# Transposing x one iteration ahead in a two-layer graph kernel

## The chip, the cores and the metric

The kernel runs on one core of a Trainium2 chip. Its time is the device time of one execution in microseconds (us); the median of several runs is given with the lowest and the highest. The engines are named as in the profile: PE is TensorE (matmuls and transposes), PEld its weight loads, DVE VectorE, ACT ScalarE, POOL GpSimd, SP SyncE. POOL and SP also issue DMAs; all data is float32 except some small index tables in bfloat16.

## The reference

```python
# x 4096 x 512, adj 4096 x 4096: about 0.2% of it and the diagonal are not zero,
# these entries lie between 0.05 and 1
a = adj + eye                                  # layer 0
d = sum(a, axis=1) ** (-0.5)
out = relu(((d[:, None] * a * d[None, :]) @ x) @ W.T + b)
x = layernorm(x + out)

adj = maximum(adj, eye)                        # layer 1: 8 heads, key size 64
q, k, v = x @ Wqs, x @ Wks, x @ Wvs            # for each head
scores = q @ k.T * 64 ** (-0.5) + 0.01 * eye - 1e16 * (1 - adj)
x = layernorm(x + sum over heads of softmax(scores) @ v @ Wo)
```

The test of the data that the kernel makes on the chip allows a shorter form. With all weights below 1, each off-diagonal score of layer 1 lies hundreds of millions below the diagonal's, so softmax is 1 on the diagonal and layer 1 is `layernorm(x + x @ (Wv @ Wo))`. With at most 9 neighbours handled as columns beside the diagonal in a row (after a redistribution in the tile), layer 0 is a sum of a few gathered rows of `y = d * (x @ W.T)`. The function that does this is `few_edges_below_one` (L420); a general path stands behind it and isn't run on this data.

## The kernel before, in words

The 4096 rows are worked on in 32 tiles of 128. Two passes follow each other.

**First pass**, the loop `for t in range(NT + 1)` (L1053 to L1095). In iteration t:

- SP loads the adjacency tile t + 3 (2 MB, `load_first` L561). 14 early tiles and the last 5 go into the 5 buffers of `big` (`a_t`) and stay until DVE has scanned them; the other 13 pass through the 2 buffers of `pn` (`a_n`), are only summed, and are loaded again later (`reload` L993).
- ACT sums the rows of tile t (`sum_rows` L710), or, for early tiles, only its negative part (L715). POOL turns the sums into `d` (`scaling`, L722 to L725); for early tiles `d` comes from DVE's scan (L970).
- x tiles are multiplied with W. `prefetch` (L1041) fetches one x tile by a POOL DMA (L550) into one of 6 buffers, `transpose_rows` (L689) transposes an x tile on PE into one of 3 PSUM buffers (`pt`), `evacuate` (L694) copies it by ACT into one of 2 buffers (`xT`), and `times` (L703) makes the product on PE into one of 5 PSUM buffers (`acc`). When `d` of that tile is known, `keep_y` (L727) scales the product on ACT (L736) and stores it to `y` in DRAM by a POOL DMA (L738).
- DVE scans an adjacency tile: 8 times MAX8 (L752) and FIND_INDEX8 (L753) on 512 columns each, 9 of its 16 steps in each iteration (`RATE`), and sorts what it found (L774 to L783). `match` (L910) hands surplus neighbours of full rows to other rows of the tile, in stages on DVE and PE: KEY, ACROSS (a transpose on PE, L855), RANKS (DVE, L864), PERM (L872), MOVE (matmuls, L881 and L884), END (DVE, L892 to L899).
- Setup steps (second-layer weights) stand between, one in an iteration that has fewer than two x tiles to turn.

The list `due` (L1031) holds for each x tile the iteration in which its product is scaled. `projected(t)` (L1027) says up to which due iteration products are made in iteration t: t + 1, and one more from each iteration in `SOONER` on. Each engine works in its own order, as the program is written out and a scheduler has laid it; some instructions are pinned to program order (ACT's `keep_y` and, in the last 7 iterations, the copies of `evacuate`).

**Second pass** (from L1101). For each tile, 9 indirect gathers on POOL (L1113, 128 rows of `y`, 256 KB each; 19 buffers, 18 ahead) fetch neighbour rows. ACT builds a scaled permutation matrix for each (`spread`, L1006 to L1019), PE multiplies and adds (L1326); in most tiles some gathers are first added together on ACT (L1130) and DVE (L1132, `presum`). Then DVE adds the own part (`scaled` L1183), applies relu and adds x (`residual` L1191), and layer 1's product and normalisation follow. Beside that DVE goes on with the scan of the reloaded tiles, and SP loads `y` and x rows (L1123) and reloads adjacency tiles.

Of the kernel before, what the change touches and what calls it, by code (L numbers as in the profile page):

```python
# [419 lines left out]
def few_edges_below_one(  # L420
# [20 lines left out]
    H, _, KD = wks.shape  # L441
    NT = N // P
# [33 lines left out]
    p1 = first.enter_context(tc.tile_pool(name="first", bufs=2))  # L476
# [71 lines left out]
    def load_x(t, engine, pool, bufs):  # L548
        x_t = pool.tile([P, D], FP, name="x_t", bufs=bufs)
        engine.dma_start(x_t, x[ts(t, P), :])  # L550
        return x_t
# [9 lines left out]
    def load_first(t, parts=1):  # L561
        if t in early or t in resident:
            return load_a(t, parts=2 if t == NT - 1 else parts)
        return load_a(t, pn, "a_n")
# [10 lines left out]
    wT = p1.tile([P, ND, D], FP, name="wT", bufs=1)  # L575
# [25 lines left out]
    def load_second_weights():  # L601

        nc.sync.dma_start(
            wv.rearrange("p (h f) -> p h f", h=H),
            wvs.rearrange("h (p j) k -> p h (j k)", j=ND),
        )
        su1 = p1.tile([P, 2, ND, D], FP, name="wo", bufs=1)
        nc.sync.dma_start(su1[:, 0], wo.rearrange("(r a) k o -> (a k) r o", a=2))
        return su1

    def order_second_weights():
        nc.gpsimd.tensor_copy(
            w_nat.rearrange("p j (h k) -> p j h k", h=H),
            wv.rearrange("p (h j k) -> p j h k", h=H, j=ND),
        )
# [70 lines left out]
    def transpose_rows(src, dcs=range(ND)):  # L686
        pt = ps_t.tile([P, 512], FP, name="pt")
        for dc in dcs:
            nc.tensor.transpose(pt[:, ts(dc, P)], src[:, ts(dc, P)], ident)  # L689
        return pt  # L690

    def evacuate(pool, name, pt, pinned=False):
        dst = pool.tile([P, ND, P], FP, name=name, bufs=2)
        copy = nc.scalar.copy(dst.rearrange("p c s -> p (c s)"), pt[:, :D])  # L694
        if pinned:
            tc.keep_in_program_order(copy)
        return dst

    def times(srcT, w, u=None, dcs=range(ND)):
        if u is None:  # L700
            u = ps_a.tile([P, D], FP, name="acc")
        for dc in dcs:
            nc.tensor.matmul(  # L703
                u, srcT[:, dc, :], w[:, dc, :], start=(dc == 0), stop=(dc == ND - 1)
            )
        return u

    def sum_rows(dst, part):
        dump = wk_.tile([P, N], mybir.dt.uint8, name="dump")
        nc.scalar.activation(dump[:, : part.shape[1]], part, AF.Copy, accum_out=dst)  # L710

    def sum_negative(t, a_t, halves=(0, 1)):
        dump = wk_.tile([P, N], mybir.dt.uint8, name="dump")
        o = slice(halves[0] * N // 2, (halves[-1] + 1) * N // 2)
        nc.scalar.activation(  # L715
            dump[:, o], a_t[:, o], AF.Relu, scale=-1.0,
            accum_out=neg_all[:, t, halves[0] : halves[0] + 1],
        )

    def scaling(t, more=None):  # L720
        deg = small.tile([P, 1], FP, name="deg")
        nc.gpsimd.tensor_scalar(deg, deg_all[:, t : t + 1], 1.0, None, op0=ALU.add)  # L722
        if more is not None:
            nc.gpsimd.tensor_tensor(deg, deg, more, ALU.add)
        nc.gpsimd.tensor_tensor(d_all[:, t : t + 1], deg, mhalf, ALU.pow)  # L725

    def keep_y(t, u):  # L727
        if t in due_first:
            y_t = p1.tile([P, D], FP, name="y_t", bufs=4)
        else:  # L730
            if not y_bank:
                y_bank.append(p1.tile([P, 8, D], FP, name="wo", bufs=1))
            y_t = y_bank[0][:, y_count[0] % 8]
            y_count[0] += 1
        tc.keep_in_program_order(
            nc.scalar.activation(y_t, u, AF.Copy, scale=d_all[:, t : t + 1])  # L736
        )
        nc.gpsimd.dma_start(y[ts(t, P), :], y_t)  # L738
# [171 lines left out]
    def match(*stages):  # L910
        for stage in stages:
            n = staged[stage]
            if stage == KEY:
                ready = n < len(sorted_)
            elif stage == PERM:
                ready = n < staged[RANKS] and n - staged[MOVE] < 2
            else:
                ready = n < staged[stage - 1]
            if stage == ACROSS:
                ready = ready and n == staged[RANKS]  # L920
            if stage == MOVE:
                ready = ready and n == staged[END]
            if not ready:
                continue
            t = order[n]
            e = edges[t]
            if stage == KEY:
                e["key"] = match_key(t)
            elif stage == ACROSS:
                e["pk"] = match_across(e["key"])  # L930
            elif stage == RANKS:
                e["rank"] = match_ranks(e["key"], e["pk"])
            elif stage == PERM:
                e["perm"] = match_perm(e["rank"])
            elif stage == MOVE:
                e["pm"] = match_move(e["rec"], e["perm"])
            else:
                match_end(t, e["pm"])
                matched.add(t)
            staged[stage] += 1  # L940
# [44 lines left out]
    def some(upto):  # L985
        while count[0] < upto:
            count[0] += 1
            next(work, None)
# [33 lines left out]
    xs, us = {}, {}  # L1022
    DEEP = 3
    RATE = 9
    SOONER = (17, 21, 25)

    def projected(t):  # L1027

        return t + 1 + sum(t >= e for e in SOONER)

    due = [(t + 1, t) for t in range(NT) if t not in early]  # L1031
    for n, t in enumerate(early):
        at = max(t + 3, -(-STEPS * (n + 1) // RATE) + 1)
# [7 lines left out]
    def prefetch(count):  # L1041
        for _ in range(count):
            if fetch:
                t = fetch.pop(0)
                xs[t] = load_x(t, nc.gpsimd, p1, 6)

    prefetch(5)
    for t in range(1, DEEP):
        a_tiles[t] = load_first(t)
# [2 lines left out]
    setup, left = iter(()), None  # L1052
    for t in range(NT + 1):  # L1053
        if t == 0:
            su1 = load_second_weights()
        if t + DEEP < NT:
            a_tiles[t + DEEP] = load_first(t + DEEP)
        if t == 3:
            order_second_weights()
            setup = second_weights(su1)  # L1060

        lo, hi = projected(t - 1) + 1, projected(t)
        ahead = [j for at, j in due if lo <= at <= hi]
        pts = []
        for j in ahead:
            prefetch(1)
            pts.append(transpose_rows(xs.pop(j)))
        kind, begin, end = next(setup, (None,) * 3) if len(ahead) < 2 else (None,) * 3
        got = begin() if kind == "t" else None
        if t < NT:  # L1070
            if t in early:
                sum_negative(t, a_tiles[t])
            else:
                sum_rows(deg_all[:, t : t + 1], a_tiles[t][:, : N // 2 if t == NT - 1 else N])
                more = None
                if t == NT - 1:
                    more = small.tile([P, 1], FP, name="more")
                    sum_rows(more, a_tiles[t][:, N // 2 :])
                scaling(t, more)
            if t in again:  # L1080
                del a_tiles[t]
        if left:
            left()
            left = None
        for j in [j for at, j in due if at == t]:
            keep_y(j, us.pop(j))
        for j, pt in zip(ahead, pts):
            us[j] = times(evacuate(p1, "xT", pt, t >= NT - 7), wT)
        if kind == "t":
            end(got)  # L1090
        if kind == "p":
            left = lambda end=end, pa=begin(): end(pa)
        if t < NT - 5:
            match(*ALL)
        some((t + 1) * RATE)  # L1095
# [170 lines left out]
    yo, zs, hs, pts, hTs, ws, sts, mats, halves = ({} for _ in range(9))  # L1266
# [28 lines left out]
    for i in range(NT + 2):  # L1295
# [6 lines left out]
        for k in range(KH):  # L1302
            ends = p == NT - 1
            t = at("T", i, k)
            if t not in (None, NT - 1):
                hTs[t] = evacuate(p2, "hT", transpose_rows(hs[t]))
            t = at("M", i, k)
# [48 lines left out]
            t = at("Q", i, k)  # L1356
# [3 lines left out]
            t = at("V", i, k)  # L1360
# [4 lines left out]
            t = at("F", i, k)  # L1365
# [45 lines left out]
```

## Time and profile before

| what | us |
|---|---|
| median of 3 runs | 639.45 (638.96 to 639.71) |
| the profiled execution | 641.63 |
| its span in the trace | 639.8 |
| busy PE / DVE / ACT / POOL | 529.4 / 556.3 / 498.3 / 357.6 |
| first gather of the second pass starts | 228.90 |
| mean granted clock of PE | 0.947 |

The profiled execution is 2.2 us above the median of the runs. In timelines a line has start, duration, engine, line of the kernel, operation, output and inputs, number of instructions put together, and in brackets the idle time before it with what ended it. In windows a line has the stretch, its length, busy time and number of instructions on PE, PEld, DVE, ACT and POOL, PE's granted clock, the share of time that the 16 DMA engines are busy, and GB/s.

### The profile page before, as it was taken

The page shows a single profiled execution, that of the slowest core. Times are in us where ns is not written, and L with a number is a line of the kernel's source. Part 1 is how long each engine was busy: PE and PEld are TensorE (multiplying, and loading weights), DVE is VectorE, ACT ScalarE, POOL GpSimd, SP SyncE. Part 2 cuts the span into 40 slices and gives each one's busy share as a digit, 9 for nine tenths or more (in the row PEclk, how much of TensorE's full clock was granted, in tenths as well). Part 3 has the DMA queues.
Part 4 walks back from the last instruction along what each step waited for, and adds up shares of the span by engine and source line. Part 5 has one row for each costly group of instructions (what it writes and reads, how often), then busy time and mean ns, then how long its engine had stood idle before and what let it go on. Part 6 is the DMA issues. An engine that isn't in the chain of part 4 may idle for free. (4 is left out here: it accounts for less than half of the span.)

```text
span 639.8 us, 7790 instructions
## 1 busy us (share of the span) xinstructions
PE 529.4 (83%) x1537; PEld 241.9 (38%) x1537; DVE 556.3 (87%) x2037; ACT 498.3 (78%) x1093; POOL 357.6 (56%) x465
## 2 busy tenths in 40 slices
PE   1599876589896636898897989999999999988884
PEld 1354333244443212344333433444444444433332
DVE  5699999999999995899988989999999999644431
ACT  0868667798876877699878888898998999857732
POOL 5222222232432167777777757676777777777730
PEclk9999987799998859799997989999999999989998
DMA  9999999899999378999999999999999888887851
GB/s 329 402 422 422 423 425 427 319 422 422 425 427 417 136 250 257 341 397 397 399 396 399 399 400 384 373 325 341 381 366 292 279 245 298 274 271 247 280 160 38
DMA packets 57273, 217.68 MB, mean 340 GB/s; under 512 B 8701, under 2 KB 9981, under 8 KB 52864
## 3 DMA queue, kind: packets, MB, share of 16 engines
q1 hardware_dynamic: 23888, 115.48, 45.6%
q0 software_dynamic: 28192, 92.30, 41.0%
q10 hardware_dynamic: 5136, 9.31, 3.9%
q8 instruction: 14, 0.23, 0.2%
q14 instruction: 43, 0.35, 0.1%
HBM read 200.28 MB, written 16.78 MB: 339 GB/s over the span
## 5 line engine op out<-in xcount | busy, mean ns | idle before, releaser
L1113 POOL DMA_INDIRECT g<-y,cols_all x288 | 287.3, 998 | 101.9 <-issue 46.2
L1326 PE MATMUL acc<-g,s_t 128*128 128x512 f32 x450 | 222.1, 625 | 31.4 <-DMA x_t<-in_x_dram 14.6
L752 DVE MAX8 v_all<-a_t 128x8 f32<-128x512 f32 x256 | 166.9, 681 | 14.8 <-DMA a_t<-in_adj_dram 14.8
L753 DVE FIND_INDEX8 idx<-v_all,a_t 128x8 uint32<-128x512 f32 x256 | 173.7, 687 | 0.0
L703 PE MATMUL acc<-wT,xT 128*128 128x512 f32 x256 | 124.9, 641 | 26.4 <-ACT xT L694 26.4
L1326 PEld LDWEIGHTS acc<-g,s_t 128*128 128x128 f32 x450 | 83.1, 197 | 122.7 <-issue 75.3
L703 PE MATMUL acc<-wvo,hT 128*128 128x512 f32 x256 | 116.9, 598 | 3.2 <-ACT hT L694 2.3
L715 ACT ACTIVATE dump<-a_t 128x2048 uint8<-128x2048 f32 (+1 forms) x50 | 119.1, 2383 | 0.0
L703 PEld LDWEIGHTS acc<-wT,xT 128*128 128x128 f32 x256 | 50.8, 206 | 88.6 <-issue 57.3
L703 PEld LDWEIGHTS acc<-wvo,hT 128*128 128x128 f32 x256 | 48.6, 192 | 65.5 <-issue 57.1
L1006 ACT ACTIVATE sq<-cols,wr_all 128x128 f32<-128x128 f32 x160 | 58.7, 393 | 15.1 <-DMA a_t<-in_adj_dram 12.8
L1132 DVE SCALAR_TENSOR_TENSOR g<-g,wr_all 128x512 f32<-128x512 f32 x58 | 43.2, 745 | 29.4 <-ACT g L1130 17.4
L1010 ACT ACTIVATE s_t<-sq,wr_all 128x128 f32<-128x128 f32 x128 | 58.3, 485 | 0.5
L722 POOL TENSOR_SCALAR deg<-deg_all 128x1 f32<-128x1 f32 x32 | 7.2, 227 | 90.9 <-DVE deg_all L970 52.2
L710 ACT ACTIVATE dump<-a_n 128x4096 uint8<-128x4096 f32 x13 | 47.2, 3634 | 0.0
L1130 ACT ACTIVATE g<-g,wr_all 128x512 f32<-128x512 f32 x31 | 22.1, 714 | 29.7 <-DMA g<-y,cols_all 22.5
L550 POOL DMA_DIRECT2D x_t<-in_x_dram x32 | 18.0, 563 | 41.3 <-PE pt L689 31.9
L783 DVE MAX8 top<-key 128x8 f32<-128x64 f32 x192 | 36.0, 214 | 0.1
L694 ACT COPY xT<-pt 128x512 f32<-128x512 f32 x32 | 18.4, 593 | 19.2 <-PE pt L689 12.4
L774 DVE SCALAR_TENSOR_TENSOR key<-key,top 128x64 f32<-128x64 f32 x128 | 32.3, 274 | 0.0
L689 PE MATMUL pt<-ident,x_t 128*128 128x128 f32 x128 | 19.9, 289 | 9.4 <-DMA x_t<-in_x_dram 8.9
L1183 DVE SCALAR_TENSOR_TENSOR h<-yo,own_all,acc 128x512 f32<-128x512 f32 (+1 forms) x33 | 23.7, 719 | 4.0 <-PE acc L1140 4.0
(135 smaller groups left out, 660.8 us busy)
## 6 DMA issues: line engine op xcount, KB each, us to landing
a_t<-in_adj_dram SPq DMA_DIRECT2D x17, 2048.0 KB, 20.1
a_t<-in_adj_dram SPq DMA_DIRECT2D x56, 512.0 KB, 14.2
a_n<-in_adj_dram SPq DMA_DIRECT2D x13, 2048.0 KB, 14.4
x_t<-in_x_dram POOLq DMA_DIRECT2D x32, 256.0 KB, 11.3
yo<-y SPq DMA_DIRECT2D x32, 256.0 KB, 5.8
x_t<-in_x_dram SPq DMA_DIRECT2D x32, 256.0 KB, 6.6
out_dram<-r_t ACTq DMA_DIRECT2D x31, 256.0 KB, 4.9
y<-y_t POOLq DMA_DIRECT2D x18, 256.0 KB, 10.8
```

What stands on the lines that cost most here:

```text
L703: nc.tensor.matmul(u, srcT[:, dc, :], w[:, dc, :], start=(dc == 0), stop=(dc == ND - 1))
L710: nc.scalar.activation(dump[:, : part.shape[1]], part, AF.Copy, accum_out=dst)
L715: nc.scalar.activation(dump[:, o], a_t[:, o], AF.Relu, scale=-1.0, accum_out=neg_all[:, t, halves[0] : halves[0] + 1],)
L752: long.append(lambda o=o, seg=seg: nc.vector.max(v[:, o], seg))
L753: long.append(lambda o=o, seg=seg: nc.vector.max_index(idx[:, o], v[:, o], seg))
L774: return lambda: nc.vector.scalar_tensor_tensor(out, a, sc, b, op0=op0, op1=op1, **kw)
L783: return lambda: nc.vector.max(top[:, f, r * 8 : r * 8 + 8], keyf[:, f])
L1006: nc.scalar.activation(sq, cols1, AF.Square, bias=wr[:, 2, k : k + 1])
L1010: nc.scalar.activation(s_t[:, k, :], away(), AF.Relu, scale=wr[:, 3, k : k + 1], bias=wr[:, 1, k : k + 1],)
L1113: nc.gpsimd.indirect_dma_start(out=slots[j], out_offset=None, in_=y[:, :], in_offset=bass.IndirectOffsetOnAxis(ap=cols_all[:, t, k : k + 1 ...
L1132: nc.vector.scalar_tensor_tensor(g, slots.pop(i * KH + k), w, g, op0=ALU.mult, op1=ALU.add)
L1326: nc.tensor.matmul(zs[i], mats[i][:, KH if k < summed[i] > 1 else k, :], slots.pop(i * KH + k), start=False, stop=(k == KH - 1),)
```

## The change

`SOONER` becomes (13, 16, 19): the product runs two, three and four due iterations ahead from iterations 13, 16 and 19 on, instead of 17, 21 and 25. From iteration 14 (`LEAD`) on, a tile of x is transposed one iteration before the one in which it is copied and multiplied: `turn_rows` is called where the transposes stood (up to 3 transposed tiles in hand) and again behind the iteration's products (up to 2 in hand). Each transpose still fetches one more x tile. What is multiplied in an iteration is still set by `projected(t)`.

```diff
-    SOONER = (17, 21, 25)
+    SOONER = (13, 16, 19)
...
+    LEAD = 14
+    turned, done = {}, [0, 0]
+
+    def turn_rows(upto, most):
+
+        while done[0] < upto and done[0] - done[1] < most:
+            j = due[done[0]][1]
+            prefetch(1)
+            turned[j] = transpose_rows(xs.pop(j))
+            done[0] += 1
...
-        lo, hi = projected(t - 1) + 1, projected(t)
-        ahead = [j for at, j in due if lo <= at <= hi]
-        pts = []
-        for j in ahead:
-            prefetch(1)
-            pts.append(transpose_rows(xs.pop(j)))
-        kind, begin, end = next(setup, (None,) * 3) if len(ahead) < 2 else (None,) * 3
+        ahead = sum(at <= projected(t) for at, _ in due)
+        turn = sum(at <= projected(t + (t >= LEAD)) for at, _ in due)
+        turn_rows(turn, 3)
+        kind, begin, end = next(setup, (None,) * 3) if ahead - done[1] < 2 else (None,) * 3
...
-        for j, pt in zip(ahead, pts):
-            us[j] = times(evacuate(p1, "xT", pt, t >= NT - 7), wT)
+        while done[1] < ahead:
+            j = due[done[1]][1]
+            us[j] = times(evacuate(p1, "xT", turned.pop(j), t >= NT - 7), wT)
+            done[1] += 1
+        turn_rows(turn, 2)
```

Written out, the x tiles multiplied in each iteration, and those transposed in it after the change, are:

| iteration | products before | products after | transposes after |
|---|---|---|---|
| 13 | 11 | 11, 14 | 11, 14 |
| 14 | 14 | 13 | 13, 16 |
| 15 | 13 | 16 | 15, 18 |
| 16 | 16 | 15, 18 | 17 |
| 17 | 15, 18 | 17 | 20 |
| 18 | 17 | 20 | 19, 22 |
| 19 | 20 | 19, 22 | 21 |
| 20 | 19 | 21 | 24 |
| 21 | 22, 21 | 24 | 23 |
| 22 | 24 | 23 | 26 |
| 23 | 23 | 26 | 25, 27 |
| 24 | 26 | 25, 27 | 28 |
| 25 | 25, 27, 28 | 28 | 29 |
| 26 | 29 | 29 | 30 |
| 27 | 30 | 30 | 31 |
| 28 | 31 | 31 | |

In the changed kernel lines behind the loop of the first pass have a number that is 11 higher. The products held in PSUM until their `d` is known are at most 5, the number of buffers, in both: in iterations 25 to 27 before, 24 to 27 after.

## The prediction

> **What bounds the kernel now.** I read the busy tenths of the whole span first, then the timelines of PE, ACT, POOL and DVE where the first pass ends (183 to 268 us), then the windows of the second pass, and last the list of waits.
>
> The busy tenths in 40 slices (16 us each) show three regimes:
>
> ```profile
> DVE  5699999999999995899988989999999999644431
> ...
> DMA  9999999899999378999999999999999888887851
> GB/s 329 402 422 422 423 425 427 319 422 422 425 427 417 136 250 257 341 397 397 399 396 399 399 400 384 373 325 341 381 366 292 279 245 298 274 271 247 280 160 38
> ```
>
> DVE is full to slice 14 (240 us) and the DMA engines to slice 12. In slice 13 (208 to 224 us) the DMA engines have almost nothing to do (136 GB/s), and from slice 16 to 25 they are full again. So the DMA engines stand empty just before the stretch in which they are the limit. What keeps them empty is the end of the first pass. PE's timeline (start, duration, what, and the idle time before it with its releaser):
>
> ```profile
> 203.86 1.09 PE L689 MATMUL pt<-ident,x_t 128*128 128x128 f32 x4 [3.08 <-DMA x_t<-in_x_dram]
> 204.74 12.95 PE L703 MATMUL acc<-wT,xT 128*128 128x512 f32 x24
> ...
> 235.02 10.33 PE L1326 MATMUL acc<-g,s_t 128*128 128x512 f32 x17 [14.56 <-DMA x_t<-in_x_dram]
> ```
>
> The last tile of x arrives at 203.8; behind its transpose three whole products (24 matmuls) run in one block to 217.7. ACT pays for that block:
>
> ```profile
> 204.96 1.26 ACT L736 ACTIVATE wo<-acc,d_all 128x512 f32<-128x512 f32 x2
> 210.91 0.58 ACT L694 COPY xT<-pt 128x512 f32<-128x512 f32 x1 [4.70 <-PE acc L703]
> 211.39 3.62 ACT L710 ACTIVATE dump<-a_t 128x4096 uint8<-128x4096 f32 x1
> ...
> 224.80 0.69 ACT L736 ACTIVATE wo<-acc,d_all 128x512 f32<-128x512 f32 x1 [0.44 <-POOL d_all L725]
> ```
>
> The copy at 210.91 needs one of two xT buffers, so it waits 4.70 us for PE, and in ACT's order the row sums of tiles 29, 30 and 31 stand behind it. From 211.39 ACT has no gap to 224.36. The gathers need the last y rows:
>
> ```profile
> 225.78 0.54 POOL L738 DMA_DIRECT2D y<-wo  x1 [0.42 <-ACT wo L736]
> 228.90 1.07 POOL L1113 DMA_INDIRECT g<-y,cols_all  x1 [2.58 <-DMA y<-wo]
> ```
>
> After that, however, the second pass doesn't wait for gathers first, it waits for DVE:
>
> ```profile
> 246.88 0.74 DVE L1132 SCALAR_TENSOR_TENSOR g<-g,wr_all 128x512 f32<-128x512 f32 x1
> ...
> 256.61 1.29 DVE L752 MAX8 v_all<-a_t 128x8 f32<-128x512 f32 x2 [6.48 <-DMA a_t<-in_adj_dram]
> ...
> 263.35 0.75 DVE L1132 SCALAR_TENSOR_TENSOR g<-g,wr_all 128x512 f32<-128x512 f32 x1 [0.98 <-DMA g<-y,cols_all]
> ```
>
> DVE comes to its first work of the second pass at 246.2, with no idle before it; PE's tile 1 waits for it and starts at 247.68. Three windows (length; busy PE, PEld, DVE, ACT, POOL; PE clock, DMA share, GB/s):
>
> ```profile
> 212.00:228.00 16.00, 6.78 (x17) 2.43 (x15) 16.00 (x40) 15.53 (x22) 4.89 (x11) 0.75 0.19 73
> ...
> 276.00:300.00 24.00, 22.38 (x66) 9.75 (x64) 23.59 (x104) 23.59 (x66) 17.64 (x19) 1.00 1.03 396
> ```
>
> In 212 to 228 the DMA share is 0.19. In the five windows from 276 to 396 it is 1.03 and PE is idle 1.62, 1.88, 5.50, 1.62 and 1.19 us, 11.8 in all, behind work that waits for gathers and for reloaded adjacency tiles (the waits list has 12.8 us of ACT L1006 on reloads). From 408 to 540 PE is busy in every microsecond of the windows, and from 540 to 616 POOL's gathers are (58.12 of 76, the rest being its issue gaps).
>
> **What the skill says.** "DMA: Bandwidth & Descriptors", section "Issuing engines are not separate DMA queues": DMAs of SP, ACT and GpSimd run on the same 16 DMA engines and interleave. The trace agrees: the last x load is issued on POOL at 177.01, while SP's adjacency tiles fill the engines, and takes 26.7 us for 256 KB; a y store in the empty stretch (225.78) lets its reader go 2.58 us later. "TensorE: Matmul & The Clock Gate", section "What's actually happening": PE runs at half clock after an idle window of about 3.4 us and needs as long of work to come back. The trace agrees: eight matmuls of a product take 3.60 to 3.70 us warm, but 5.10, 6.66 and 5.38 after idle times of 3.27, 4.96 and 6.89. "Perfetto Trace Analysis", section "Optimization Strategy": where a kernel has several regimes, interleaving them may help. That is how I read an emptier DMA stretch filled from a later, full one; no trace shows yet whether it pays here.
>
> **The change, part by part.**
>
> *Amount of work.* Nothing is added or taken away: 32 transposes, copies, products, loads and stores on both sides. All cost lies in place and waiting.
>
> *Products earlier.* Tile 13's iteration makes two products instead of one, and from then to iteration 25 the products run one or two ahead of before. PE has room: between 85 and 137 it waits 3.27, 4.96, 0.67, 6.89 and 2.47 us (18.3), of which one product needs 3.6 to 6.7. Price zero on PE. ACT's copy of each (0.58) only changes place.
>
> *x loads earlier.* Each transpose fetches one more x tile, so the last load is issued in iteration 23 instead of 25. ACT's sums of iterations 23 and 25 start at 167.03 and 178.14, so it goes 11 us earlier, to about 166. With the same 26.7 us to land it is there at 193 instead of 203.7. PE's four waits for x_t (2.31, 1.58, 1.89 and 3.08, of which three lie after 186) go. POOL's queue is moved past, too: loads now stand ahead of some y stores, and POOL waits in place up to 3.18 us for DMAs in flight (at 180.72). A y store late by that is not on the path before the very last ones.
>
> *What is then last.* The products of tiles 29 to 31 no longer come in one block, so ACT's 4.70 goes and its gaps in 183 to 225.5 (1.22, 1.15, 1.46, 2.48, 1.40, 4.70, 0.44: 12.85) mostly too. The next thing late is the adjacency itself: the second half of tile 31 lands at 212.2. Two y stores (0.5 MB) that came later now move ahead of it: at 417 GB/s 1.2 us, so 213.4. Then its sum (1.91 and a read, 2.1): 215.5. From that sum's end (223.78) to the first gather (228.90) before took 5.1: first gather at 220.6, **8.3 us earlier**.
>
> *What that is worth.* Not 8.3. DVE isn't moved: it is busy 12.00 of 12.00 us in every window from 164 to 240, and it reaches L1183 at 246.2 in both kernels. Tile 1 still starts at 247.7, and the reload that costs DVE 6.48 is issued behind DVE's own work as before. What remains is that 8.3 / 1.25 (the issue period of gathers: 228.90, 230.27, ... 244.10) = 6.6 gathers of 256 KB, 1.74 MB, are fetched while the DMA engines were empty. The 19 gather buffers allow it: with the 6.1 and 10.8 us that tile 0 took before from first gather to its products and through them, its buffers are free by 238, before the 20th gather is due. In the full stretch 252 to 400 these 1.74 MB needn't be moved; at 396 GB/s that is **4.4 us**, less than the 11.8 that PE idles in there, so all of it can be won. The 0.98 wait at 263.35 is part of it and isn't counted twice. It is kept to the end, since PE and then POOL are dense behind it. Bounds: 0, if PE's idle comes from DVE and ACT and not from DMA; 8.3, if the whole lead carries through.
>
> *A new wait on DVE.* In the built program's order, tile 13's product and tile 16's transposes now stand ahead of rank transposes on PE, and DVE's compare (L864) one search earlier. The rank transpose of the fifth `match` ran on PE at 129.60 to 129.87, behind a product (124.38, 5.38 us at low clock), and DVE took it at 131.06; now DVE wants it at about 129.28 and gets it at 129.93: +0.65 us, on an engine that is the limit to 248, so it counts in full, with the scan, the sorting and all later searches queued behind. Bounds: 0 if the product runs warm (3.70 in place of 5.38), and up to 3 if it runs as the one of 6.66 and a transpose waits in front of it. The other moved points (L892) have 1.8 us and more of slack by my reading.
>
> *Sum*: -4.4 + 0.65 = -3.75. The profiled execution took 641.63 (span 639.8 and 1.8 around it), so 637.9; it lies 2.2 above the median of the runs, 639.45, from which the same step gives **635.7**.
>
> **Rivals.** A change of 0.2% (1.28 us) is about what measurement can tell from none here.
> - *The lead is worth nothing.* PE's idle in 276 to 396 would be a matter of ACT and DVE (88% and 94% busy there). For it: the list has 22 us of PE waits on rank_key L848, an ACT instruction. Against: ACT itself waits 12.8 on reloads there. Time: 639.45 + 0.65 - 0.98 = 639.1.
> - *Slower, by DVE waiting on PE.* DVE waits in order for rank transposes and moves (L855, L884) that now stand behind products of 3.7 to 6.7 us. With 2 to 3 us of such waits and nothing from the lead: 641.2. It decides once DVE's new waits pass what the lead brings: over 1.3 us if that is zero, over 5.7 if it is the 4.4. For it: DVE has no idle there, so each wait is a loss. Against: the matches after the fifth have slack.
> - *Half the lead.* The loads are earlier in the order, but wait on POOL for y stores and DMA slots (waits of 2.54, 2.80 and 3.18 in 177 to 187), or ACT keeps a gap. First gather 4 earlier: 4 / 1.25 = 3.2 gathers, 2.1 us at 396 GB/s, less 0.65: 638.0.
> - *All of the lead.* If reloads, too, land sooner because fewer gathers are in their way (6.48 at 256.61), 8 of the 8.3 stay: 631.4.
>
> **Chances.** Forecast 0.50 (own range 633.5 to 637.5), nothing 0.16, slower 0.12, half 0.14, all 0.08. The range 631.2 to 640.5 leaves out the worse part of the slower case and the end of the best one. Faster by over 0.2% (below 638.2): 0.50, 0.08 and two thirds of the half case, 0.67; within: 0.20; slower (above 640.7): 0.13.
>
> **What would show it.** Right: PE's waits for x_t after 186 gone; no ACT wait near 4.7 before the row sum of tile 29; the first L1113 at about 220.6; L1183 of tile 0 at 246 to 247; PE idle in 276 to 396 down from 11.8 to about 7.5; DVE's wait ahead of L864 near 130 at most 1 us. Wrong: a first gather after 226, or DVE reaching L1183 after 248, or PE's idle in the full DMA stretch unchanged while the first gather did move.

## The result, and the profile after

| | before | after |
|---|---|---|
| median of 22 runs each, us | 640.63 (638.96 to 643.14) | 637.33 (633.59 to 643.08) |
| ratio, 95% interval | | 0.9955 (0.9933 to 0.9978) |
| profiled execution (span), us | 641.63 (639.8) | 635.99 (634.2) |
| first gather starts, us | 228.90 | 221.27 |
| DVE at tile 0's `scaled`, us | 246.22 | 247.89 |

The ratio is that of the averages, 640.64 and 637.78. 0.45% of 640.63 is 2.9 us; the interval reaches from 1.4 to 4.3. The forecast was 3.75. The runs of the changed kernel lie further apart (9.5 us) than those of before (4.2), so single profiles below are read for what happened, not for a total.

First the busy tenths of the changed kernel, in 40 slices of now 15.9 us:

```profile
DVE  5699999999999997799999999999999999654431
...
DMA  8999999899999587999999999999998888887851
GB/s 328 402 419 427 421 426 427 328 415 425 427 423 422 218 283 222 376 393 395 398 398 399 400 399 389 372 343 350 364 369 282 289 243 296 279 260 237 284 160 38
```

Slice 13, the empty one, moves 218 GB/s in place of 136. That is mostly the end of the adjacency, as the slice now covers 206 to 222 us and the first gather starts at 221.27. What the gathers fill shows in a window at fixed times, 221 to 228 us, of before and then of the changed kernel; the last two numbers are the DMA share, 0.29 and then 0.91, and GB/s:

```profile
221.00:228.00 7.00, 0.00 (x0) 0.00 (x0) 7.00 (x18) 6.53 (x16) 2.12 (x5) 0.50 0.29 114
```

```profile
221.00:228.00 7.00, 0.37 (x1) 0.40 (x2) 7.00 (x17) 7.00 (x21) 5.21 (x6) 0.50 0.91 298
```

The end of the first pass on PE:

```profile
182.71 0.63 PE L689 MATMUL pt<-ident,x_t 128*128 128x128 f32 x4 [2.00 <-DMA x_t<-in_x_dram]
...
200.88 3.70 PE L703 MATMUL acc<-wT,xT 128*128 128x512 f32 x8 [1.54 <-ACT xT L694]
...
227.63 10.26 PE L1337 MATMUL acc<-g,s_t 128*128 128x512 f32 x18 [15.43 <-DMA x_t<-in_x_dram]
```

One wait for x is left, at 182.71. The last x load goes out on POOL at 166.93 (before 177.01), and the last product starts at 200.88, alone; before, three stood in one block up to 217.7. So ACT is held by something else:

```profile
201.31 3.62 ACT L710 ACTIVATE dump<-a_t 128x4096 uint8<-128x4096 f32 x1 [0.48 <-DMA a_t<-in_adj_dram]
...
207.28 3.62 ACT L710 ACTIVATE dump<-a_t 128x4096 uint8<-128x4096 f32 x1 [1.68 <-DMA a_t<-in_adj_dram]
...
214.14 1.91 ACT L710 ACTIVATE dump<-a_t 128x2048 uint8<-128x2048 f32 x1 [0.69 <-DMA a_t<-in_adj_dram]
```

Where the sum of tile 29 waited behind a copy that waited 4.70 us for PE, all three sums now wait for the adjacency tiles themselves, the last one to 214.14. POOL, 7.6 us earlier than before:

```profile
218.15 0.54 POOL L738 DMA_DIRECT2D y<-wo  x1 [0.42 <-ACT wo L736]
221.27 1.07 POOL L1124 DMA_INDIRECT g<-y,cols_all  x1 [2.58 <-DMA y<-wo]
```

DVE is the one place that became later:

```profile
131.02 0.35 DVE L864 TENSOR_SCALAR_CACHE_REDUCE above<-pt,rank_key 128x128 f32<-128x128 f32 x1 [1.54 <-PE pt L855]
...
247.89 0.75 DVE L1194 SCALAR_TENSOR_TENSOR h<-yo,own_all,acc 128x512 f32<-128x512 f32 x1
...
257.69 1.29 DVE L752 MAX8 v_all<-a_t 128x8 f32<-128x512 f32 x2 [7.41 <-DMA a_t<-in_adj_dram]
```

It waits 1.54 us for the rank transpose, and comes to tile 0's `scaled` (now L1194) 1.67 us later. PE's tile 1, which needs DVE's next instruction, starts at 249.36 in place of 247.68 after 11.36 us of idle: up to here the earlier gathers buy nothing. At tile 1's `scaled` the two kernels are level again, at 265.93 and 265.92: of DVE's three waits on the way there before (1.51 us for ACT, 6.48 for a reload, 0.98 for a gather) only the one for the reload is left. That they agree to 0.01 us is chance. The kernel before, and three runs below that differ from it only further on, reach tile 1 at 264.90 to 267.88.

The windows from tile 1's `scaled` to tile 11's, of before and then of the changed kernel (length; busy PE, PEld, DVE, ACT, POOL; PE clock, DMA share, GB/s):

```profile
265.93:397.70 131.77, 119.82 (x342) 52.53 (x340) 124.86 (x533) 116.31 (x317) 95.00 (x98) 0.96 1.03 393
```

```profile
265.92:392.30 126.38, 117.78 (x344) 51.92 (x342) 124.60 (x532) 111.30 (x304) 87.71 (x91) 0.98 1.03 397
```

Ten tiles later the changed one is 5.4 us ahead, at the same DMA share of 1.03. POOL issued 98 gathers in that stretch before and 91 after: seven fewer, which had been fetched earlier. PE is idle 8.6 us in place of 11.95, and busy 2.0 less at a clock of 0.98 in place of 0.96. From tile 11 to tile 24 it stays 5.4 ahead. How much of that is due to the earlier gather these two profiles can't tell: the table of all runs shows that the length of this stretch does not follow it. ACT's waits for gathers and for reloaded adjacency tiles do. From 250 to 400 us, before and then changed (total, times, longest):

```profile
ACT sq L1006 <- DMA a_t<-in_adj_dram: 12.8, 5, 3.3
ACT g L1130 <- DMA g<-y,cols_all: 6.8, 2, 6.4
```

```profile
ACT sq L1006 <- DMA a_t<-in_adj_dram: 6.6, 4, 2.2
```

The first is halved and the second is gone.

### The profile page after: what moved, and what is told of

Same layout as the page of the kernel before. It is cut to its first block, busy times and chain, and to the rows that moved or that the text cites. A ratio compares the mean times of both kernels' runs of the same rounds, so it can differ in the third digit from the quotient of the medians.

```text
span 634.2 us, 7789 instructions
## 1 busy us (share of the span) xinstructions
PE 525.2 (83%) x1537; PEld 240.9 (38%) x1537; DVE 555.9 (88%) x2037; ACT 497.9 (79%) x1093; POOL 358.0 (56%) x465
## 5 line engine op out<-in xcount | busy, mean ns | idle before, releaser
L1337 PE MATMUL acc<-g,s_t 128*128 128x512 f32 x450 | 218.9, 619 | 41.9 <-DVE g L1143 26.3
L1143 DVE SCALAR_TENSOR_TENSOR g<-g,wr_all 128x512 f32<-128x512 f32 x58 | 43.1, 743 | 28.3 <-DMA g<-y,cols_all 14.9
L1006 ACT ACTIVATE sq<-cols,wr_all 128x128 f32<-128x128 f32 x160 | 58.8, 393 | 8.7 <-DMA a_t<-in_adj_dram 6.6
L1141 ACT ACTIVATE g<-g,wr_all 128x512 f32<-128x512 f32 x31 | 22.1, 712 | 21.7 <-DMA g<-y,cols_all 14.7
L694 ACT COPY hT<-pt 128x512 f32<-128x512 f32 x31 | 17.9, 578 | 16.3 <-PE pt L689 15.9
L1194 DVE SCALAR_TENSOR_TENSOR h<-yo,own_all,acc 128x512 f32<-128x512 f32 (+1 forms) x33 | 23.7, 719 | 5.0 <-PE acc L1151 4.3
```

The lines of the kernel that those rows point to most:

```text
L1006: nc.scalar.activation(sq, cols1, AF.Square, bias=wr[:, 2, k : k + 1])
L1143: nc.vector.scalar_tensor_tensor(g, slots.pop(i * KH + k), w, g, op0=ALU.mult, op1=ALU.add)
L1337: nc.tensor.matmul(zs[i], mats[i][:, KH if k < summed[i] > 1 else k, :], slots.pop(i * KH + k), start=False, stop=(k == KH - 1),)
```

## The experiments

Theory: what the change gains is the earlier first gather, whose bytes leave the full DMA stretch; what it loses is DVE's wait. Rivals: the gain comes from somewhere else in the freer first pass; the full stretch is bound by engines and not by bytes; DVE's wait costs nothing. "Ratio" is that to the kernel before on the same chip, with its 95% interval.

**The raised lead of the products (`SOONER`) alone** (edit of the changed kernel, as in the runs that follow up to the gather held back)

```diff
-    LEAD = 14
+    LEAD = NT + 1
```

> Only the raised lead of the products (13, 16, 19); no transposing ahead. Theory (an earlier first gather fills the empty DMA stretch; each DVE wait ahead of it costs): tile 13's product still stands ahead of the fifth rank transpose, so DVE waits about 1.5 us at L864 again; the last x load is issued one iteration later than with both parts, lands near 199, first gather about 221 to 224; time 3 to 5 us below before in the profile, ratio 0.993 to 0.998. Rival (the transposes ahead are what unblocks ACT): first gather near 228, ratio 1.000 to 1.003.

Ratio 0.9972 (0.9953 to 0.9992). First gather 222.49; DVE waits 1.84 us at L864. As the theory has it.

**The transposes ahead alone**

```diff
-    SOONER = (13, 16, 19)
+    SOONER = (17, 21, 25)
```

> Only the transposes one iteration ahead; SOONER as before (17, 21, 25). Theory: product 14 isn't moved into iteration 13, so DVE's wait at L864 is under 0.3 us; the last x load goes one iteration earlier than before, lands near 198, but three products still fall in iteration 25; first gather about 222 to 225, ratio 0.992 to 0.997. Rival (the raised lead is what pulls the loads): first gather 227 to 229, ratio 0.999 to 1.001.

Ratio 0.9958 (0.9931 to 0.9985). First gather 221.87; no wait at L864, DVE at tile 0's `scaled` at 246.49. Three products still fall in one iteration, but start earlier, since the x tiles are there:

```profile
202.54 7.03 PE L703 MATMUL acc<-wT,xT 128*128 128x512 f32 x16
```

So both rivals written for these two runs fall: each part alone pulls the last x load forward by enough (to 173.84 and 171.96), and either alone is faster than before, by an amount whose interval holds that of the change. The two parts do the same thing, they don't add up. The wait on DVE comes with the raised `SOONER` only, from the second product of iteration 13.

**The second product of iteration 13 put later**

```diff
-    SOONER = (13, 16, 19)
+    SOONER = (14, 16, 19)
```

> SOONER (14, 16, 19) in place of (13, 16, 19), all else as in the changed kernel: the second product of iteration 13 moves to 14, behind the fifth rank transpose. Theory: no DVE wait at L864, DVE reaches tile 0's L1194 about 1.6 us earlier (246.3), first gather still about 221; 0.5 to 1.7 us below the changed kernel: ratio to before 0.992 to 0.995. Rival (DVE's 1.5 us are taken back in its later wait for a reload, so they cost nothing): same time as the changed kernel, 0.9955.

Ratio 0.9985 (0.9970 to 1.0001), outside what either theory gave. DVE's wait is gone (tile 0's `scaled` at 246.32), but the first gather is no longer at 221. PE and ACT, and then POOL, of this run:

```profile
190.09 1.09 PE L689 MATMUL pt<-ident,x_t 128*128 128x128 f32 x4 [6.14 <-DMA x_t<-in_x_dram]
```

```profile
196.60 0.58 ACT L694 COPY xT<-pt 128x512 f32<-128x512 f32 x1 [4.76 <-PE acc L703]
```

```profile
224.50 1.07 POOL L1124 DMA_INDIRECT g<-y,cols_all  x1 [2.59 <-DMA y<-wo]
```

The last x load goes at 170.69 in place of 166.93, PE waits 6.14 for a tile of x in front of products, and ACT's copy waits for those products as it did before the change. From that copy to the first gather it takes 27.90 us, in which only 0.44 us of waiting stand in ACT's row. My expectation held the first gather fixed and was wrong there.

**The second product at 15, and the lead from 16 on**

```diff
-    SOONER = (13, 16, 19)
+    SOONER = (15, 16, 19)
```

> The changed kernel with SOONER (15, 16, 19). Theory: no DVE wait at L864; the first gather is between that of (13, 16, 19), 221.3, and that of (14, 16, 19), 224.5, by how late the last x load goes; time follows DVE's arrival and the gather's start: 0.54 us for each us of the first gather (262 KB each 1.25 us at 398 GB/s is 0.53). Ratio 0.992 to 0.998.

Ratio 0.9979 (0.9963 to 0.9995). First gather 225.98, DVE 246.41, no wait at L864. The gather is later than with 14, not between the two as I wrote. The last x load isn't later (170.04), but ACT's copy waits longer for PE, 6.90 us, and starts at 198.08. From there to the first gather it takes 27.90 us again.

```diff
-    SOONER = (13, 16, 19)
+    SOONER = (16, 19, 22)
```

> The changed kernel with SOONER (16, 19, 22): transposes ahead from 14 on, but no second product near the fifth rank transpose. Theory: no DVE wait at L864 (DVE at tile 0's L1194 by 246.5), first gather 221 to 222.5, since each part alone reaches that: 0.5 to 1.7 us below the changed kernel, ratio to before 0.991 to 0.995. Rival (the wait is taken back later): equal to the changed kernel within 0.2%.

Ratio 0.9940 (0.9917 to 0.9962). No wait, DVE at 246.28, first gather 223.44 (later than the 221 to 222.5 expected). ACT's last wait for a product ends at 195.54 here, and the first gather is once more 27.90 us behind. So in these three runs the first gather follows ACT's last wait for PE, and not the time of the last x load, which is about the same in all (170.69, 170.04 and 170.45). The ratio is the lowest of all variants of the change, but its interval overlaps that of the change.

**The changed kernel again**, on the chip of the two runs before

> The changed kernel once more, on the same chip as the other runs of this set, to compare with: ratio to before 0.9955 as before (0.993 to 0.998).

Ratio 0.9967 (0.9945 to 0.9988). First gather 220.95. DVE's wait is 0.62 here and not 1.54. PE of this run, and then of the first profile of the same kernel:

```profile
124.50 5.40 PE L703 MATMUL acc<-wT,xT 128*128 128x512 f32 x8 [4.28 <-ACT xT L694]
129.74 0.27 PE L855 MATMUL pt<-ident,rank_key 128*128 128x128 f32 x1
```

```profile
124.56 6.32 PE L703 MATMUL acc<-wT,xT 128*128 128x512 f32 x8 [3.75 <-ACT xT L694]
130.71 0.27 PE L855 MATMUL pt<-ident,rank_key 128*128 128x128 f32 x1
```

The product in front of the rank transpose starts at the same time and takes 5.40 or 6.32, and DVE waits 0.9 us more in the second case. PE's granted clock in 128 to 130 us was 0.80 and 0.54. In the kernel before the same product took 5.38, and 5.21, 5.76 and 6.28 in three runs that differ from it only later. "TensorE: Matmul & The Clock Gate", section "What's actually happening", says that the window by which the clock is raised runs freely, so that the change of clock falls differently from run to run; the two profiles of one program agree with that.

**The first gather held back**

```diff
-                    sum_rows(more, a_tiles[t][:, N // 2 :])
+                    for n in range(5):
+                        sum_rows(more, a_tiles[t][:, N // 2 :])
```

> The changed kernel with ACT summing the second half of tile 31 five times in place of once (8.3 us more, same value), so that the last y row and the first gather come as late as before (about 229), while DVE, PE and the x loads stay as changed. Theory: the gain is gone and DVE's 1.5 us at L864 stay: ratio 0.999 to 1.004. Rival (the gain comes from something else, such as PE's or ACT's freer first pass or the order of reloads): ratio about 0.9955 to 0.998.

Ratio 1.0017 (1.0001 to 1.0033): the gain is gone, and some is lost, though the x loads, the products and PE's order are the changed ones. First gather 229.09. ACT's waits from 250 to 400 us are back, too (12.1 us for reloads, 5.6 for gathers). From tile 1 to tile 11:

```profile
265.07:396.06 130.99, 117.16 (x342) 51.54 (x340) 125.39 (x533) 115.64 (x316) 96.74 (x99) 0.99 1.03 396
```

The edit delays ACT's own work behind the last sum as well. But ACT stands idle before its first gathered tile (L1141) for 7.09 us in the changed kernel and 7.36 here, so it isn't short of that time, and the rival of a freer first pass falls.

**Bytes where DMA is empty, and where it is full** (of the kernel before)

```diff
         some((t + 1) * RATE)
+    for n in range(11):
+        junk = p1.tile([P, D], FP, name="x_t", bufs=6)
+        nc.sync.dma_start(junk[:, :320], x[ts(n, P), :320])
     first.close()
```

> The kernel before with 11 loads more of 128 x 320 numbers (1.80 MB, as much as 6.9 gathers) on SP right behind the last adjacency tile, where the DMA engines stand empty (212 to 228 us); nothing reads them. Theory: they cost nothing or nearly so, ratio 0.999 to 1.002 (the first own rows of y stand behind them on SP but wait for the y stores anyway). Rival (each byte costs its time wherever it lies): 4.5 us, ratio 1.007.

```diff
                 load_own(i + 2)
+                if 3 <= i < 14:
+                    seen = small.tile([P, 1], FP, name="seen")
+                    nc.gpsimd.tensor_scalar(seen, junk[:, :1], 1.0, None, op0=ALU.add)
+                if 2 <= i < 13:
+                    junk = p2.tile([P, 320], FP, name="junk", bufs=1)
+                    nc.sync.dma_start(junk, x[ts(i, P), :320])
```

> The kernel before with the same 11 loads of 128 x 320 numbers (1.80 MB) on SP, one in each of the second pass's tiles 2 to 12, where the DMA share is 1.0, each read by a small POOL instruction a tile later (11 of some 0.22 us). Theory: the bytes are on the path there: 1.80 MB at 398 GB/s is 4.5 us, ratio 1.005 to 1.009, and PE's idle between 276 and 400 grows by about that. Rival (PE, ACT and DVE bound that stretch): ratio 0.999 to 1.002.

These two ran on another chip, on which the kernel before takes 707.71 and not 640. In the gap: ratio 0.9982 (0.9953 to 1.0011), so 1.80 MB cost at most 0.8 us there. But on that chip DVE comes to tile 0's `scaled` only at 269.76, 23.5 us later than above, which could hide a cost; the run wasn't made on a chip like the first. In the full stretch: 1.0126 (1.0063 to 1.0190). Once more on a chip like the first:

> The kernel before with 1.80 MB of loads in the full stretch once more, now on a chip where before takes about 640: in the first try before itself took 707.7. Theory: +4.5 us, ratio 1.005 to 1.009. Rival (PE, ACT and DVE bound that stretch): 0.999 to 1.002.

Ratio 1.0255 (1.0221 to 1.0289), 16 us, more than three times the 4.5 estimated for the bytes, though the DMA share fell to between 0.89 and 0.97 from 276 to 372 us. The waits of 250 to 410 us say why (total, times, longest):

```profile
ACT sq L1006 <- DMA a_t<-in_adj_dram: 27.9, 7, 7.0
...
POOL seen L1356 <- DMA junk<-in_x_dram: 7.9, 4, 3.5
...
POOL seen L1356 <- DVE ints L780: 5.1, 1, 5.1
...
POOL seen L1356 <- DVE key L774: 4.1, 1, 4.1
```

The small reading instruction that I put on POOL waits in POOL's order for 17.1 us, with all gathers behind it, and ACT's waits for reloads rise from 12.8 (250 to 400 us, before) to 27.9. The probe cost more than what it was to measure. Neither of the two runs prices bytes; I tried it the other way round.

**Fewer bytes, in the full stretch and after it** (of the kernel before)

```diff
+        if 5 <= i < 12:
+            xs[i] = xs[i - 1]
+            return
         xs[i] = load_x(t, nc.sync, p2, 3)
```

> The kernel before without the x loads of the second pass's tiles 5 to 11 (7 times 256 KB, 1.84 MB, issued in the full DMA stretch); these tiles add tile 4's x rows instead, so their output isn't the reference's. No instruction and no wait is added. Theory (the full stretch is bound by bytes): 1.84 MB at 398 GB/s is 4.6 us, ratio 0.991 to 0.995, and PE's idle of 11.8 us between 276 and 396 falls by about that. Rival (it is bound by PE, ACT and DVE, and the changed kernel gains for another reason): ratio 0.999 to 1.001.

Ratio 0.9935 (0.9911 to 0.9959), 4.2 us for 1.84 MB, where 4.6 were expected. The sums over the five windows from 276 to 396, of before, this run and the changed kernel:

```profile
sum 120.00, PE 108.20 PEld 47.65 DVE 113.16 ACT 105.05 POOL 85.98; mean PE 21.64 PEld 9.53 DVE 22.63 ACT 21.01 POOL 17.20
```

```profile
sum 120.00, PE 112.05 PEld 49.56 DVE 116.50 ACT 110.64 POOL 88.35; mean PE 22.41 PEld 9.91 DVE 23.30 ACT 22.13 POOL 17.67
```

```profile
sum 120.00, PE 109.89 PEld 48.78 DVE 118.31 ACT 110.15 POOL 83.25; mean PE 21.98 PEld 9.76 DVE 23.66 ACT 22.03 POOL 16.65
```

All of PE, DVE and ACT get more done in the same 120 us once bytes are taken out; PE's idle falls from 11.8 to 7.95, and ACT's 12.8 us of waits for reloads are gone. Only 1.7 us of waiting were put down to the x loads themselves in that stretch before, so it is not a wait for x that went.

```diff
+        if 21 <= i < 28:
+            xs[i] = xs[i - 1]
+            return
         xs[i] = load_x(t, nc.sync, p2, 3)
```

> As the run before, but without the x loads of tiles 21 to 27 (issued from about 490 us on, where the DMA share is 0.84 to 0.86 and PE and POOL are dense); these tiles add tile 20's x rows instead. Theory: nothing, ratio 0.998 to 1.001. Rival (each byte is worth its time wherever it lies): 0.993.

Ratio 0.9977 (0.9957 to 0.9998), 1.5 us, more than the theory's none, since 1 lies outside the interval; the rival's 0.993 lies outside, too. So the same bytes are worth about a third there (1.5 of 4.2 us) of what they are worth in the full stretch. In its profile this kernel is 2.6 us ahead of before at tile 11, where the two programs don't differ yet, and 2.2 at the end; where its 1.5 us arise this profile doesn't show. PE's idle from 276 to 396 is 10.4 in it, and 11.8 before: that is the scatter of one program's profiles.

**All runs by one formula.** Lead is 228.90 less the first gather; 262,144 bytes each 1.25 us at 396 GB/s make it worth an estimated 0.53 us for each us. Delay is DVE's arrival at tile 0's `scaled` less 246.22. Estimated gain: 0.53 lead - delay; the ratio from it is 1 less gain / 640.6. The last two columns are ACT's waits for gathers and reloads together from 250 to 400 us (L1006 and L1130, or the lines that took their place), and the time from tile 1's `scaled` to tile 11's; before has 19.6 and 131.8.

| run | lead | delay | gain | ratio from it | measured | ACT's waits | tile 1 to 11 |
|---|---|---|---|---|---|---|---|
| changed | 7.63 | 1.67 | 2.4 | 0.9963 | 0.9955 (0.9933 to 0.9978) | 6.6 | 126.4 |
| changed again | 7.95 | 0.69 | 3.5 | 0.9945 | 0.9967 (0.9945 to 0.9988) | 7.2 | 127.1 |
| raised lead alone | 6.41 | 2.27 | 1.1 | 0.9982 | 0.9972 (0.9953 to 0.9992) | 6.2 | 126.8 |
| transposes ahead alone | 7.03 | 0.27 | 3.5 | 0.9946 | 0.9958 (0.9931 to 0.9985) | 7.1 | 131.3 |
| (14, 16, 19) | 4.40 | 0.10 | 2.2 | 0.9965 | 0.9985 (0.9970 to 1.0001) | 15.1 | 129.8 |
| (15, 16, 19) | 2.92 | 0.19 | 1.4 | 0.9979 | 0.9979 (0.9963 to 0.9995) | 14.9 | 131.2 |
| (16, 19, 22) | 5.46 | 0.06 | 2.8 | 0.9956 | 0.9940 (0.9917 to 0.9962) | 8.3 | 131.1 |
| gather held | -0.19 | 0.80 | -0.9 | 1.0014 | 1.0017 (1.0001 to 1.0033) | 17.7 | 131.0 |

Seven of eight lie in their intervals, one of them at its edge. Without the delay, the raised lead alone (0.9947), the changed kernel again (0.9934) and (14, 16, 19) lie outside. That speaks for charging DVE's delay in full, but no pair of runs shows it by itself: lead and delay differ from profile to profile, and the runs that remove the wait also moved the gather. Nor do the ratios establish the size of 0.53: one ratio of 0.9965 for all runs but the last would lie in five of the other seven intervals.

ACT's waits fall with the lead: 14.9 and more up to a lead of 4.4, at most 8.3 from 5.46 on (15.3 in the profile of the run with fewer bytes late, which is the kernel before up to there). The stretch from tile 1 to tile 11 does not: it took 131.3 with transposes ahead alone, at a lead of 7.03, and 126 to 127 only in the three profiles in which DVE also comes to tile 0 late with an early gather. Those three executions are also 1.3 to 2.4 us faster than the medians of their kernels. Why the stretch was shorter in them stays open.

## Why the prediction was right, and where its sizes were off

- *What limits the end of the first pass.* Right. The last x load was to go at 166 and went at 166.93; PE's waits behind 186 are gone, and so is ACT's wait of 4.70. The last half tile was to be there at 213.4 (ACT takes it at 214.14), the first gather at 220.6 (221.27, and 220.95 in the second profile). One wait for x of 2.00 us, before 186, is left. From the end of the last sum to the first gather it takes 5.1 us in both kernels.
- *The lead is not worth itself but its bytes.* Right in the main. With the gather held the gain is gone; a lead of 7.63 brought 2.9, and at most 4.3. With 1.84 MB less in the full stretch the kernel before gains 4.2 us by itself, and ACT's 12.8 us of waits for reloads are gone there, as they are down to 6.2 to 7.6 with leads of over 5 us. That the lead acts by its bytes, and not by the fuller buffers as such, is argued from this; no run separates the two in the changed kernel. That bytes cost nothing in the gap rests on one run on the slower chip. PE's 11.36 us of idle ahead of tile 1 shows that the lead is not used where it arises.
- *4.4 us for it.* Mis-sized a little: the lead was 7.63, not 8.3, which gives 4.0. How much each profile shows of that scatters: 5.4 ahead at tile 11 in the changed kernel, 1.2 with transposes ahead alone. PE's idle in 276 to 396 was to fall to about 7.5; it was 10.1, and 11.1 in the second profile. It was a bad sign to name: with the gather held it is 13.8, with (15, 16, 19), at a lead of only 2.92, it is 8.7, and the kernel before itself has 11.8 or 10.4. The removal of bytes came to 7.95.
- *The wait at L864.* Right in place and mechanism, mis-sized in the first profile. 0.65 forecast; 0.62 in two profiles (the changed kernel again, the gather held), 1.54 and 1.84 in two others, all within the bounds of 0 and 3. The step took the product at 5.38, from one profile; in the four profiles with this wait it takes 5.40 to 6.62, by when PE's clock comes back. With it, DVE reached tile 0's `scaled` at 247.89, where 246 to 247 was named as the sign of being right and 248 as that of being wrong; the second profile has 246.91.
- *The sum.* With the measured lead and delay it is 2.4 us in the first profile and 3.5 in the second; measured were 2.9 and 2.1 (0.9967 of 641.68), so that the two come in the other order, within their intervals. How near the sum comes to one measurement is in part luck, as the delay alone differs by 1.0 between two profiles of one program.
- *Tile 1 at 247.7.* It started at 249.36, by that wait.
- *The parts.* The prediction costed them as one. Alone, either part gains (0.9972 and 0.9958), which the list of products per iteration doesn't tell: what counts is that ACT's last waits for PE end early enough. The last x load alone doesn't settle it: with the raised `SOONER` alone it goes out at 173.84 and the first gather comes at 222.49, with (15, 16, 19) at 170.04 and 225.98.
- *The level.* 635.7 was worked from a median of 639.45 of three runs; in the longer set the median of before is 640.63, which accounts for 1.2 of the 1.6 us between 635.7 and 637.33.
- *Rivals.* A worthless lead (639.1) and a slower kernel (641.2) had as their deciding points a gain from the lead of zero, and DVE waits greater than what the lead brings; neither came about. The 641.2 is 1.75 above 639.45, less than the 2 to 3 us of waits that it names. And of the 22 us of waits on rank_key held up for the first rival, 13.9 are PEld's; PE itself waited 8.4. The run with the gather held is the nearest to the second: no lead, DVE 0.8 later, 1.0017.

## What to carry to other kernels

Where a transfer can start earlier but its reader can't, ask what the engines that move it are doing now and later: it pays by its bytes if they leave a stretch in which DMA is the limit for one in which it is idle, here by an estimated 0.53 us for each us of lead, and not by the time of the lead. An order that puts a matmul group ahead of a small transpose which another, fully busy engine waits for costs that engine the rest of the group, and if PE has just been idle, the group's length varies from run to run. A probe that adds an instruction to an in-order queue measures that queue; taking bytes away measured bytes. And look for a sign that follows the cause over several profiles: here the waits of one engine for DMA did, while PE's idle time in fixed windows and the length of one stretch did not.

## What the runs showed that was not expected

One program's product of eight matmuls, begun at 124.4 to 124.6 in each profile after 2.9 to 4.3 us of PE idle, took 5.40, 5.40 and 6.32 us (two profiles of the changed kernel, one with only the last sums repeated); the kernel before, too, had it at 5.21 to 6.28, after 6.89 us of idle each time. The changed kernel's 22 runs lie 9.5 us apart, before's 4.2; by how much that product explains it was not tried. And the chips differ: the same kernel before took 640.9, 641.7 and 641.2 us on three sets and 707.71 on a fourth; in the run with bytes in the gap there, the first gather still starts at 228.01, DVE is 23.5 us late at tile 0, and the windows from 408 to 616 us move 225 to 304 GB/s with PE idle in them, where before moved 267 to 355 with PE mostly full. Why was not tried.
